# Six expert blocks of a routed layer begun among the last batches' routing, and the blocks' PSUM banks kept in one tile

## The chip, the cores and the metric

The kernel runs on one core of a Trainium2 chip. The metric is the device time of one execution in microseconds. A core has five engines with a queue each: TensorE (PE) for matrix products, with its weight loads (PEld) beside it, VectorE (DVE), ScalarE (ACT), GpSimd (POOL) and SyncE (SP), which issues most DMA transfers. The engines wait for each other by semaphores: a waiting instruction holds everything behind it in its queue. PE's products land in PSUM, which this kernel uses as eight banks of 512 fp32 values per partition; ScalarE and VectorE fetch them from there.

## The reference

A decoder of two layers on x of shape 32 x 100 x 256, each layer with self-attention, cross-attention to a context of 361 rows and a feed-forward part, each followed by a layer normalisation. What matters here is the last part: eight experts, of which each token uses the one with the highest gate.

```python
logits = x_flat @ Wg + bg                       # 3200 tokens, 8 experts
probs = softmax(logits); assignments = argmax(probs)
h = gelu(einsum('nd,edh->neh', x_flat, W1) + b1)
eo = einsum('neh,ehd->ned', h, W2) + b2
selected = take_along_axis(eo, assignments[:, None, None], axis=1)[:, 0, :]
out = probs[token, assignment] * selected
x = layernorm(x + out)
```

## The kernel before

**Slots.** The two layers of attention are planned by hand in slots. `at(slot, place, do)` (L397) files a piece of work under a slot and a place in it, and `run_slots` (L746) issues everything in that order: the scores of the step two slots ahead, then the places -1 and 0, the three turnings of the next step with the places 1, 2, 3 between them, and the sums that close the slot. The order in which instructions are issued is each engine's queue order. A batch of the second layer starts its cross-attention every five slots (`starts`, L467): batch 23 in slot 298, batch 31, the last, in slot 338.

**Routing.** When a batch of the second layer is through its cross-attention, its rows are turned (`r_x_m`), the router gives its logits (L589), and in groups of four batches (at the end two, one, one) VectorE finds each token's expert, counts the tokens of each expert so far (`sofar`, L695) and gives each token a row in a DRAM buffer, `regions`, with one region per expert (L706 to L708). POOL makes the row an integer (L717) and scatters the batch's rows there (L712). The slots of these steps stand in `ROUTING` (L26): for batches 20 to 23 the scatters are in slots 314 to 317, for the last batch in slot 347.

**Blocks.** After the last slot, `block_table` (L727) counts how many blocks of 128 tokens each expert needs and writes for each of 32 blocks its first row in `regions` and its expert into `table`. SP, PE and VectorE read it into registers (`of_four`, L854). Blocks are a software pipeline (L925): in step i, SP asks for the rows and the first matrix of block i + 10 (`xb`, 129 KB, L869; `wb`, 257 KB, L871), PE turns block i + 2 (L877) and ScalarE copies the turned rows to SBUF (`bxT`, L879); PE multiplies block i + 1 by the first matrix (L887), ScalarE applies bias and gelu (`bhT`, L890); PE multiplies block i by the second matrix (L896); VectorE adds bias and residual and takes mean and variance (L899 to L903). ScalarE normalises block i - 3 (L915), POOL scatters it to the output (L712). The last two blocks are normalised on VectorE. The turned rows (`bt`), first products (`bh`) and second products (`bo`) are tiles of the PSUM pool `ps_m`, two of each, opened after the attention's pools are closed:

```python
ps = ps_m.tile([P, NC2, P], F32, tag="t", name=f"bt_{i}")     # L875
ps = ps_m.tile([P, NC2, P], F32, tag="h", name=f"bh_{i}")     # L883
ps = ps_m.tile([P, D], F32, tag="o", name=f"bo_{i}")          # L894
```

A tile is also what waits are made from: the layer that records the program adds a wait wherever an instruction touches a tile that another engine used before.

Of the kernel before, what the change touches and what calls it, by code (L numbers as in the profile page):

```python
# [10 lines left out]
F32 = mybir.dt.float32  # L11
# [7 lines left out]
E = 8  # L19
# [14 lines left out]
FILLS = 23  # L34
NO_TOKEN = 1000000
# [29 lines left out]
def decoder_kernel(ctx: ExitStack, tc: tile.TileContext, a: dict, out: bass.AP):  # L65
# [5 lines left out]
    x_all = state.tile([S, B, ROW], F32, name="x_all")  # L71
    xs = [x_all[:, b, :D] for b in range(B)]
# [3 lines left out]
    table = state.tile([32, 64], I32, name="table")  # L76

# [14 lines left out]

    def centre_and_scale(dst, src, scale):
        nc.vector.tensor_scalar(dst, src, scale[0], scale[1], ALU.subtract, ALU.mult)

    with ExitStack() as att:
# [3 lines left out]
        ps_s = att.enter_context(tc.tile_pool(name="ps_s", bufs=1, space=bass.MemoryType.PSUM))  # L100
        ps_r = att.enter_context(tc.tile_pool(name="ps_r", bufs=4, space=bass.MemoryType.PSUM))
        att.enter_context(tc.manual_schedule())

        def bank(tag):
            return ps_r.tile([P, 512], F32, tag="r", name=f"r_{tag}")
# [12 lines left out]
        nc.vector.tensor_copy(x_all[:, :, D + 1].bitcast(I32), ids)  # L118
# [159 lines left out]

        def score_banks(tag):
            return ps_s.tile([P, NG, 512], F32, tag="s", name=f"sc_{tag}")  # L280
# [376 lines left out]
        place = const.tile([S, B], I32, name="place")  # L657

# [25 lines left out]
        def shares(first, n):  # L684

            top = x_all[:, first:first + n, D]
            nc.vector.tensor_reduce(top, routed["lg"], AX.X, ALU.add)
            nc.vector.reciprocal(top, top)
# [13 lines left out]
        def rows_of(first, n):  # L702
# [5 lines left out]
            nc.vector.tensor_reduce(row[:, first:first + n], ahead, AX.X, ALU.add)  # L708

# [6 lines left out]
        def send(b):  # L716
            nc.gpsimd.tensor_copy(place[:, b:b + 1], row[:, b:b + 1])  # L717
            scatter("regions", out=regions, out_offset=bass.IndirectOffsetOnAxis(ap=place[:, b:b + 1], axis=0),
                    in_=x_all[:, b, :])
# [7 lines left out]
        def block_table():  # L727


            ps = bank("counts")[:, :E]  # L730
            nc.tensor.matmul(ps, lhsT=share_of_block, rhs=sofar, start=True, stop=True)
            n = sm.tile([P, E], F32, tag="tb_n", name="tb_n")
            nc.vector.tensor_scalar(n, ps, 0.5 - 0.5 / P, ROUND, ALU.add, ALU.add)
            nc.vector.tensor_scalar(n, n, ROUND, float(P), ALU.subtract, ALU.mult)
            upto = sm.tile([P, E], F32, tag="tb_upto", name="tb_upto")
            nc.vector.tensor_tensor_scan(upto, ones[:, :E], n, 0.0, ALU.mult, ALU.add)
            past = sm.tile([32, E - 1], F32, tag="tb_past", name="tb_past")
            col = sm.tile([32, 2], F32, tag="tb_col", name="tb_col")
            nc.vector.tensor_scalar(past, upto[:32, :E - 1], c["steps"][:32, 0:1], None, ALU.is_le)
            nc.vector.tensor_reduce(col[:, 1:2], past, AX.X, ALU.add)  # L740
            nc.vector.tensor_scalar(n, n, -1.0, float(B * S), ALU.mult, ALU.add)
            nc.vector.tensor_tensor_reduce(past, past, n[:32, :E - 1], 1.0, c["steps"][:32, 0:1], ALU.mult, ALU.add, col[:, 0:1])
            nc.vector.tensor_copy(rows_by_block[:, 0:64:32], col)
            nc.vector.transpose(table, rows_by_block)

# [79 lines left out]
        b2 = xnT.rearrange("p k b s -> p (k b s)")[:, :E * D].rearrange("p (e d) -> p e d", e=E)  # L825
# [10 lines left out]
        block_table()  # L836

    with ExitStack() as moe:
# [5 lines left out]
        ps_m = moe.enter_context(tc.tile_pool(name="ps_m", bufs=2, space=bass.MemoryType.PSUM))  # L844
        moe.enter_context(tc.manual_schedule())

        y_all = mw.tile([P, BLOCKS, D], F32, name="y_all")
        mv_all = mw.tile([P, BLOCKS, 2], F32, name="mv_all")
        rs_all = mw.tile([P, BLOCKS], F32, name="rs_all")
        shift = mw.tile([P, BLOCKS], F32, name="shift")  # L850
        blocks = [{} for _ in range(BLOCKS)]
        ENG = mybir.EngineType

        def of_four(i, what, engines, most):  # L854

            i += 32 * what
            return nc.values_load_multi_w_load_instructions(
                table[0:1, i:i + 4], engines=engines, min_val=0, max_val=most,
                skip_runtime_bounds_check_because="the table's rows and experts are within these bounds for any counts")[1]

        def load_block(i):
            if i % 4 == 0:
                firsts = of_four(i, 0, (ENG.SP,), (BLOCKS_AT_MOST - 1) * P)
                experts = of_four(i, 1, (ENG.SP, ENG.PE, ENG.DVE), E - 1)
                for t, first, e in zip(blocks[i:i + 4], firsts, experts):
                    t["first"], t["e"] = first, e
            t = blocks[i]
            t["x"] = m16.tile([P, ROW], F32, tag="xb", name=f"xb_{i}")
            nc.sync.dma_start(t["x"], regions[bass.ds(t["first"], P), :])  # L869
            t["w"] = m12.tile([P, WROW], F32, tag="wb", name=f"wb_{i}")  # L870
            nc.sync.dma_start(t["w"], a["experts_1"][bass.ds(t["e"], 1)].rearrange("o p n -> (o p) n"))  # L871

        def turn_block(i):
            t = blocks[i]
            ps = ps_m.tile([P, NC2, P], F32, tag="t", name=f"bt_{i}")  # L875
            for k in range(NC2):
                nc.tensor.transpose(ps[:, k, :], t["x"][:, k * P:(k + 1) * P], ident)  # L877
            t["xT"] = m2.tile([P, NC2, P], F32, tag="bxT", name=f"bxT_{i}")
            nc.scalar.copy(t["xT"], ps)  # L879

        def first_layer(i):
            t = blocks[i]
            ps = ps_m.tile([P, NC2, P], F32, tag="h", name=f"bh_{i}")  # L883
            t["hT"] = m2.tile([P, NC2, P], F32, tag="bhT", name=f"bhT_{i}")
            for m in range(NC2):
# [39 lines left out]
        for i in range(-10, BLOCKS):  # L925
            for f, d in ((load_block, 10), (turn_block, 2), (first_layer, 1)):
                if 0 <= i + d < BLOCKS:
                    f(i + d)
# [89 lines left out]
```

## Time and profile before

| | |
|---|---|
| median of three runs | 1750.93 us (1747.35 to 1752.39) |
| the profiled execution | 1748.03 us |
| its span | 1745.9 us |
| PE busy | 1681.2 us, 96% |
| DVE, ACT, POOL busy | 74%, 52%, 63% |
| last scatter to `regions` issued | at 1658.23 us |
| first turning of a block on PE | at 1663.51 us |
| second product of block 0 and of block 30 | at 1669.67 and 1728.78 us |

The time lies a little above the span because work around the first and last instruction is in it. The profile has several views. The view by stretch gives for each stretch the busy time of each engine and the granted clock of TensorE (1.00 is full speed). The chain that ended last is followed back from the last instruction, each step to what released it. The timeline gives instructions in order of time: start, length, engine, line, operation, output<-inputs, count, and in brackets how long the engine had been idle and what released it. Lines in it are those of the kernel before.

### The profile page before, as it was taken

How to read it: one execution, taken by the hardware profiler on the slowest of the kernel's cores; microseconds unless marked ns; L12 is line 12 of the kernel's file. 1: busy time of each engine (PE TensorE's matmuls, PEld its weight loads, DVE VectorE, ACT ScalarE, POOL GpSimd, SP SyncE). 2: the span in 40 equal slices, each digit the busy share in tenths (PEclk: the TensorE clock that was granted, in tenths of full speed). 3: DMA queues.
4: the chain of work that ended last, by engine and by line, in shares of the span. 5: the costliest groups of instructions: out<-in, count | busy, mean ns of one | idle time of the engine just before them, and what ended most of it. 6: DMA issues, size and time to landing. Idle time of an engine off the chain costs nothing. (4 is left out here: it accounts for less than half of the span.)

```text
span 1745.9 us, 52245 instructions
## 1 busy us (share of the span) xinstructions
PE 1681.2 (96%) x20801; PEld 1302.3 (75%) x20801; DVE 1291.6 (74%) x3784; ACT 912.9 (52%) x2252; POOL 1096.9 (63%) x1657
## 2 busy tenths in 40 slices
PE   8999999999999999999999999999999999999786
PEld 6777777777777777776777777777777777777575
DVE  5677777777777777777667787877777787777655
ACT  3455555555555555555445555555555555554354
POOL 1566666666566666666237667776767667675646
PEclk9999999999999999999999999999999999999888
DMA  4001322332233233310421132000100000100083
GB/s 160 14 22 30 81 76 54 85 81 64 70 81 84 48 82 81 76 30 22 160 63 55 55 103 65 19 20 19 28 19 21 18 22 26 37 27 18 18 257 113
DMA packets 64047, 104.90 MB, mean 60 GB/s; under 512 B 6107, under 2 KB 43485, under 8 KB 63678
## 3 DMA queue, kind: packets, MB, share of 16 engines
q1 hardware_dynamic: 59790, 94.44, 19.7%
q0 software_dynamic: 3584, 6.59, 1.2%
q8 instruction: 165, 2.70, 0.7%
q14 instruction: 76, 0.62, 0.1%
q10 hardware_dynamic: 432, 0.54, 0.1%
HBM read 61.32 MB, written 41.13 MB: 59 GB/s over the span
## 5 line engine op out<-in xcount | busy, mean ns | idle before, releaser
L364 POOL TENSOR_TENSOR pr<-pr,mx_x 100x361 f32<-100x361 f32 x992 | 766.3, 802 | 230.9 <-DVE mx_x L360 222.1
L375 ACT ACTIVATE pT_x<-r_t_x 120x400 f32<-120x400 f32 (+1 forms) x768 | 370.6, 503 | 271.2 <-PE r_t_x L374 269.2
L374 PEld LDWEIGHTS r_t_x<-ident,pr 100*120 100x120 f32 (+1 forms) x3072 | 313.7, 138 | 112.5 <-POOL pr L364 34.0
L374 PE MATMUL r_t_x<-ident,pr 100*120 100x100 f32 (+1 forms) x3072 | 380.7, 252 | 12.3 <-POOL pr L364 11.1
L360 DVE CUSTOM_DVE_ANT_0 pr<-sc_x,dist 100x361 f32<-100x361 f32 x512 | 244.7, 530 | 121.8 <-PE sc_x L277 97.7
L360 DVE CUSTOM_DVE_ANT_0 pr<-sc_x,zero 100x361 f32<-100x361 f32 x512 | 244.6, 530 | 76.7 <-PE sc_x L277 69.5
L277 PE MATMUL sc_x<-kT_x,qz_x 32*100 32x361 f32 x2048 | 221.8, 502 | 8.5 <-DVE mx_x L360 5.2
L89 POOL TENSOR_SCALAR rs_s<-mv_s 100x1 f32<-100x1 f32 x64 | 14.3, 224 | 289.7 <-DVE mv_s L87 261.6
L389 PE MATMUL r_a_x<-pT_x,v_cross 120*32 120x100 f32 (+1 forms) x6144 | 172.2, 252 | 0.0
L318 DVE TENSOR_REDUCE mx_s<-sc_s 100x16 f32<-100x1600 f32 x64 | 116.6, 1823 | 69.8 <-PE sc_s L277 69.8
L477 ACT ACTIVATE kT_x<-r_k,c_columns 128x361 f32<-128x361 f32 x128 | 72.0, 563 | 162.2 <-PE r_k L475 162.2
L389 PEld LDWEIGHTS r_a_x<-pT_x,v_cross 120*32 120x32 f32 (+1 forms) x6144 | 129.9, 110 | 24.1 <-ACT kT_s L424 2.1
L332 ACT ACTIVATE pT_s<-r_t_s 100x400 f32<-100x400 f32 x256 | 112.7, 504 | 30.2 <-PE r_t_s L331 27.6
L321 DVE TENSOR_TENSOR pr_s<-sc_s,mx_s 100x1600 f32<-100x1600 f32 x64 | 116.8, 1824 | 2.2
L331 PE MATMUL r_t_s<-ident,pr_s 100*100 100x100 f32 x1024 | 107.3, 251 | 0.3 <-DVE pr_s L321 0.3
L277 PEld LDWEIGHTS sc_x<-kT_x,qz_x 32*100 32x100 f32 x2048 | 68.3, 160 | 45.2 <-issue 13.8
L484 PE MATMUL r_v<-shared,ctx 128*120 128x256 f32 (+1 forms) x384 | 100.5, 384 | 0.0
L331 PEld LDWEIGHTS r_t_s<-ident,pr_s 100*100 100x100 f32 x1024 | 95.2, 130 | 5.5 <-ACT shared L486 0.6
L486 ACT COPY v_cross<-r_v 120x256 f32<-120x256 f32 x168 | 62.5, 372 | 58.0 <-PE r_v L484 58.0
L268 DVE SCALAR_TENSOR_TENSOR qz_x<-r_qx,qm_x_scale,qm_x_bias 128x400 f32<-128x400 f32 x64 | 37.6, 629 | 71.8 <-PE r_qx L257 71.8
L475 PE MATMUL r_k<-ctx,shared 128*128 128x361 f32 x256 | 88.6, 468 | 1.1 <-DMA ctx<-in_ctxT_dram 1.1
L475 PE MATMUL r_k<-ctx,c_l1x_wk 128*128 128x361 f32 x256 | 89.2, 470 | 0.0
(220 smaller groups left out, 2910.6 us busy)
## 6 DMA issues: line engine op xcount, KB each, us to landing
regions<-no_token SPq DMA_DIRECT2D x23, 1161.0 KB
ctx<-in_ctxT_dram SPq DMA_DIRECT2D x64, 361.0 KB
wb<-in_experts_dram SPq DMA_DIRECT2D x32, 257.0 KB
values_dram<-shared SPq DMA_DIRECT2D x8, 768.0 KB
v_cross<-values_dram SPq DMA_DIRECT2D x8, 768.0 KB
dist<-in_dist_dram SPq DMA_DIRECT2D x32, 141.0 KB
xb<-regions SPq DMA_DIRECT2D x32, 129.0 KB
x_all<-in_x_dram SPq DMA_DIRECT2D x32, 100.0 KB
```

The costliest lines, as they stand in the source:

```text
L277: nc.tensor.matmul(dst, lhsT=qz[rows, p, k, :], rhs=kT[rows, k, :], start=True, stop=True)
L318: nc.vector.tensor_reduce(mx, sg, AX.X, ALU.max)
L321: nc.vector.tensor_tensor(pr, sg, mx.unsqueeze(3).to_broadcast([S, NG, NG, S]), ALU.subtract)
L331: nc.tensor.transpose(pt[:, j, :], t["pr_s"][:, j, g, :], ident[:S, :S])
L332: nc.scalar.activation(t["pT_s"][:, g], pt, AF.Exp)
L360: nc.vector.tensor_tensor_reduce(pr[:, j, :SK], sc[:, j, :], bias, 1.0, LOWEST, ALU.add, ALU.max, mx)
L364: nc.gpsimd.tensor_tensor(pr[:, j, :SK], pr[:, j, :SK], mx.to_broadcast([S, SK]), ALU.subtract)
L374: nc.tensor.transpose(pt[:n, j, :], t["pr_x", g][:, j, k0:k0 + n], ident[:S, :S])
L375: nc.scalar.activation(t["pT_x", g][:n, i], pt[:n], AF.Exp)
L389: nc.tensor.matmul(av[32 * j:32 * j + 32, h, :], lhsT=t["v_x"][:n, i, head(part, j), :], rhs=t["pT_x", part][:n, i, j, :], start=(i == 0), ...
L475: nc.tensor.matmul(ps, lhsT=c[sx + "_wk"][:, k, m * P:(m + 1) * P], rhs=t["ctx"][:, k, :], start=(k == 0), stop=(k == NC2 - 1))
L484: nc.tensor.matmul(ps, lhsT=ctx_b[:, k, k0:k0 + n], rhs=c[sx + "_wv"][:, k, :], start=(k == 0), stop=(k == NC2 - 1))
```

## The change

Six blocks (`BEGUN`) are begun before the attention is over. After batch 23's counting (slot 313), a first table is made of six full blocks among the tokens of the first 24 batches (`table_of_begun`). SP loads their rows and first matrices in slots 321 to 326, one block a slot, into places of `x_all` and `xnT` that are no longer needed (`x_all` now has 128 partitions). Their turnings and first products are put at the places in `BEGINNING`, in slots 338 to 347, in banks of the attention's pool; ScalarE adds the bias there without the gelu. PE and VectorE read their experts' registers in slot 346. After the last slot come the table of the other blocks (`table_of_others`, counted behind the begun ones), then six gelus and six second products (`end_begun`) and the sums (`sum_begun`). Then the pipeline runs over the other 26 blocks. Three of the begun blocks are normalised by ScalarE and stored ahead of block 6's second product, three by VectorE between the blocks' stores.

The attention's two PSUM pools stay open for the blocks. One tile of four banks, `score_banks("blocks")`, holds the turnings (banks 0 and 1) and the first products (banks 2 and 3) of all 26 blocks. Second products take the four rotating banks of the other pool. For the single batches 30 and 31 the row number is made an integer by VectorE, and POOL writes a small constant in its place.

```diff
+BEGUN, BEGIN_WITH = 6, 24
+BEGINNING = (((338, 1), (340, 2)), ((338, 3), (342, 1)), ((339, 1), (343, 3)), ((339, 3), (345, 2)), ((340, 1), (346, 0)), ((341, 1), (347, 1)))
...
-    x_all = state.tile([S, B, ROW], F32, name="x_all")
-    xs = [x_all[:, b, :D] for b in range(B)]
+    x_all = state.tile([P, B, ROW], F32, name="x_all")
+    xs = [x_all[:S, b, :D] for b in range(B)]
...
+    words = xnT.rearrange("p k b s -> p (k b s)")
+    b2 = words[:, :E * D].rearrange("p (e d) -> p e d", e=E)
+    w1_begun = words[:, E * D:E * D + BEGUN * WROW].rearrange("p (i d) -> p i d", i=BEGUN)
...
+    def load_rows_of_block(t):
+        nc.sync.dma_start(t["x"], regions[bass.ds(t["first"], P), :])
+    def load_matrix_of_block(t):
+        nc.sync.dma_start(t["w"], a["experts_1"][bass.ds(t["e"], 1)].rearrange("o p n -> (o p) n"))
+    def turn_rows(t, ps):
+        for k in range(NC2):
+            nc.tensor.transpose(ps[:, k, :], t["x"][:, k * P:(k + 1) * P], t["ident"])
+        nc.scalar.copy(t["xT"], ps)
+    def first_matrix(t, ps, function):
+        for m in range(NC2):
+            for k in range(NC2):
+                n = k * D + m * P
+                nc.tensor.matmul(ps[:, m, :], lhsT=t["w"][:, n:n + P], rhs=t["xT"][:, k, :], start=(k == 0), stop=(k == NC2 - 1))
+        for m in range(NC2):
+            nc.scalar.activation(t["hT"][:, m, :], ps[:, m, :], function, bias=t["w"][:, NC2 * D + m:NC2 * D + m + 1])
+    def second_matrix(t, ps, w):
+        for m in range(NC2):
+            nc.tensor.matmul(ps, lhsT=t["hT"][:, m, :], rhs=w[:, bass.ds(t["e"], 1), m * D:(m + 1) * D].rearrange("p o n -> p (o n)"),
+                             start=(m == 0), stop=(m == NC2 - 1))
+    def share_and_residual(i, ps, pool):
+        t = blocks[i]
+        y = t["y"]
+        nc.vector.tensor_tensor(y, ps, b2[:, bass.ds(t["e"], 1), :].rearrange("p o d -> p (o d)"), ALU.add)
+        nc.vector.scalar_tensor_tensor(y, y, t["x"][:, D:D + 1], t["x"][:, :D], ALU.mult, ALU.add)
+        st = pool.tile([P, 6], F32, tag="st", name=f"st_{i}")
+        nc.vector.bn_stats(st, y)
+        nc.vector.bn_aggr(mv_all[:, i, :], st)
...
+    ps_s = ctx.enter_context(tc.tile_pool(name="ps_s", bufs=1, space=bass.MemoryType.PSUM))
+    ps_r = ctx.enter_context(tc.tile_pool(name="ps_r", bufs=4, space=bass.MemoryType.PSUM))
+    def bank(tag):
+        return ps_r.tile([P, 512], F32, tag="r", name=f"r_{tag}")
+    def score_banks(tag):
+        return ps_s.tile([P, NG, 512], F32, tag="s", name=f"sc_{tag}")
...
+            if n == 1:
+                nc.vector.tensor_copy(place[:, first:first + 1], row[:, first:first + 1])
...
         def send(b):
-            nc.gpsimd.tensor_copy(place[:, b:b + 1], row[:, b:b + 1])
+            if group_of(b)[1] > 1:
+                nc.gpsimd.tensor_copy(place[:, b:b + 1], row[:, b:b + 1])
+            else:
+                nc.gpsimd.memset(between, 0.0)
             scatter("regions", out=regions, out_offset=bass.IndirectOffsetOnAxis(ap=place[:, b:b + 1], axis=0),
-                    in_=x_all[:, b, :])
+                    in_=x_all[:S, b, :])
...
+        def table_of_begun():
+            assert BEGIN_WITH * S - E * (P - 1) > (BEGUN - 1) * P
+            n, upto = blocks_of_experts("begun", 0.5 / P - 0.5, None)
+            nc.vector.tensor_scalar(upto, upto, float(BEGUN), None, ALU.min)
+            nc.vector.tensor_copy(done[:, 0:1], upto[:, 0:1])
+            nc.vector.tensor_tensor(done[:, 1:], upto[:, 1:], upto[:, :E - 1], ALU.subtract)
+            nc.vector.tensor_scalar(n, done, -float(P), float(B * S), ALU.mult, ALU.add)
+            write_table("begun", upto, lambda: n, c["steps"][:, 0:1])
+            nc.vector.tensor_tensor(over, done[:, 1:], done[:, :E - 1], ALU.subtract)
+            nc.vector.tensor_scalar(over, over, float(P), float(B * S), ALU.mult, ALU.add)
+            nc.vector.scalar_tensor_tensor(first_done, done[:, 0:1], float(P), c["steps"][:, 0:1], ALU.mult, ALU.add)
+        def begun_rows():
+            firsts = of_table(0, BEGUN, 0, (ENG.SP,), (BLOCKS_AT_MOST - 1) * P)
+            experts = of_table(0, BEGUN, 1, (ENG.SP,), E - 1)
+            for i, (first, e) in enumerate(zip(firsts, experts)):
+                t = blocks[i]
+                t["first"], t["e"], t["ident"] = first, e, ident
+                t["x"], t["y"] = x_all[:, i, :], x_all[:, BEGUN + i, :D]
+                t["hT"], t["xT"] = slot_of(2 * BEGUN + i), slot_of(3 * BEGUN + i)
+                t["w"] = w1_begun[:, i, :]
+        def begun_experts():
+            for t, e in zip(blocks, of_table(0, BEGUN, 1, (ENG.PE, ENG.DVE), E - 1)):
+                t["e"] = e
+        def load_begun(i):
+            load_rows_of_block(blocks[i])
+            load_matrix_of_block(blocks[i])
+        def of_bank(name):
+            return split(bank(name)[:, :NC2 * P], NC2)
+        def plan_beginning():
+            last = starts(1, BEGIN_WITH - 1)[0]
+            at(last + 15, 1, table_of_begun)
+            at(last + 22, 3, begun_rows)
+            at(last + 48, 3, begun_experts)
+            for i, (turning, first) in enumerate(BEGINNING):
+                at(last + 23 + i, 0, lambda i=i: load_begun(i))
+                at(*turning, lambda i=i: turn_rows(blocks[i], of_bank(f"bt_{i}")))
+                at(*first, lambda i=i: first_matrix(blocks[i], of_bank(f"bh_{i}"), AF.Identity))
+        def end_begun():
+            for t in blocks[:BEGUN]:
+                nc.scalar.activation(t["hT"], t["hT"], AF.Gelu)
+                t["ps"] = bank("bo")[:, :D]
+                second_matrix(t, t["ps"], shared)
+        def sum_begun():
+            for i in range(BEGUN):
+                share_and_residual(i, blocks[i]["ps"], sm)
+                if i == BEGUN // 2 - 1:
+                    margin(0, BEGUN // 2)
+                    scale(0, BEGUN // 2)
+                if i == BEGUN // 2:
+                    shift_of(0, BEGUN // 2)
...
         run_slots()
         nc.scalar.preload_act_table_set("gelu_and_others")
-        block_table()
+        table_of_others()
+        end_begun()
+        sum_begun()
...
+        banks = score_banks("blocks")
...
+            for load in (load_matrix_of_block, load_rows_of_block) if i == BEGUN else (load_rows_of_block, load_matrix_of_block):
+                load(t)
...
         def turn_block(i):
             t = blocks[i]
-            ps = ps_m.tile([P, NC2, P], F32, tag="t", name=f"bt_{i}")
-            for k in range(NC2):
-                nc.tensor.transpose(ps[:, k, :], t["x"][:, k * P:(k + 1) * P], ident)
+            t["ident"] = ident
             t["xT"] = m2.tile([P, NC2, P], F32, tag="bxT", name=f"bxT_{i}")
-            nc.scalar.copy(t["xT"], ps)
+            turn_rows(t, banks[:, i % 2, :NC2 * P].rearrange("p (k s) -> p k s", k=NC2))
         def first_layer(i):
             t = blocks[i]
-            ps = ps_m.tile([P, NC2, P], F32, tag="h", name=f"bh_{i}")
             t["hT"] = m2.tile([P, NC2, P], F32, tag="bhT", name=f"bhT_{i}")
-            for m in range(NC2):
-                for k in range(NC2):
-                    nc.tensor.matmul(ps[:, m, :], lhsT=t["w"][:, k * D + m * P:k * D + (m + 1) * P], rhs=t["xT"][:, k, :],
-                                     start=(k == 0), stop=(k == NC2 - 1))
-            for m in range(NC2):
-                nc.scalar.activation(t["hT"][:, m, :], ps[:, m, :], AF.Gelu, bias=t["w"][:, NC2 * D + m:NC2 * D + m + 1])
+            first_matrix(t, banks[:, 2 + i % 2, :NC2 * P].rearrange("p (k s) -> p k s", k=NC2), AF.Gelu)
         def second_layer(i):
-            t = blocks[i]
-            ps = ps_m.tile([P, D], F32, tag="o", name=f"bo_{i}")
-            for m in range(NC2):
-                nc.tensor.matmul(ps, lhsT=t["hT"][:, m, :], rhs=shared[:, bass.ds(t["e"], 1), m * D:(m + 1) * D].rearrange("p o n -> p (o n)"),
-                                 start=(m == 0), stop=(m == NC2 - 1))
-            y = y_all[:, i, :]
-            nc.vector.tensor_tensor(y, ps, b2[:, bass.ds(t["e"], 1), :].rearrange("p o d -> p (o d)"), ALU.add)
-            nc.vector.scalar_tensor_tensor(y, y, t["x"][:, D:D + 1], t["x"][:, :D], ALU.mult, ALU.add)
-            st = m4.tile([P, 6], F32, tag="st", name=f"st_{i}")
-            nc.vector.bn_stats(st, y)
-            nc.vector.bn_aggr(mv_all[:, i, :], st)
...
+        half = BEGUN // 2
+        for i in range(BEGUN - 10, BLOCKS):
             for f, d in ((load_block, 10), (turn_block, 2), (first_layer, 1)):
-                if 0 <= i + d < BLOCKS:
+                if BEGUN <= i + d < BLOCKS:
                     f(i + d)
-            if 2 < i:
+            if i == BEGUN - 1:
+                for j in range(half):
+                    normalise_on_scalar(j)
+                    store(j)
+            if i < BEGUN:
+                continue
+            if i > BEGUN + 2:
                 normalise_on_scalar(i - 3)
-            if i < 0:
-                continue
             second_layer(i)
             if i == BLOCKS - 1:
                 normalise_on_scalar(i - 2)
                 store(i - 3)
+            if i == BEGUN + 1:
+                margin(half, half)
+                scale(half, half)
             if i % 2:
                 margin(i - 1, 2)
                 scale(i - 1, 2)
-            elif i:
+            elif i > BEGUN:
                 shift_of(i - 2, 2)
-            if 2 < i < BLOCKS - 1:
+            if BEGUN + 1 < i < BEGUN + 2 + half:
+                normalise(i - 2 - half)
+                store(i - 2 - half)
+            if BEGUN + 2 < i < BLOCKS - 1:
                 store(i - 3)
         store(BLOCKS - 3)
```

## The prediction

> **What bounds the kernel now.** I read the share of busy time first (TensorE, PE, 96% of 1745.9 us), then the busy time by stretch, then the chain that ended last, then the rows of one block, then the waits in the built program of each kernel. By stretch (columns: stretch, length, busy PE, weight load, DVE, ACT, POOL with instruction counts, granted TensorE clock, DMA share, GB/s):
>
> ```profile
> 1640.00:1650.00 10.00, 7.34 (x91) 5.61 (x89) 6.70 (x32) 3.64 (x11) 5.17 (x9) 0.94 0.01 2
> 1650.00:1660.00 10.00, 2.80 (x13) 2.24 (x13) 5.36 (x33) 1.82 (x3) 4.27 (x7) 0.50 0.13 36
> 1660.00:1670.00 10.00, 5.21 (x25) 4.79 (x26) 0.00 (x0) 1.92 (x7) 0.00 (x0) 0.54 0.76 207
> 1680.00:1690.00 10.00, 10.00 (x72) 9.22 (x72) 7.91 (x24) 7.42 (x22) 8.29 (x10) 1.00 0.86 259
> ```
>
> Up to about 1640 us PE is full. From 1645 to 1665 it is half idle at half clock: the last batch's routing is a chain of small steps. Then 32 expert blocks run with PE full again. The change wants to fill the hole with six of these blocks. The chain (start, length, what):
>
> ```profile
> 1658.23 2.82 DMA regions<-x_all,place
> ...
> 1662.75 2.65 DMA xb<-regions
> ...
> 1669.67 0.86 PE bo L896 x4
> 1670.54 0.22 PE bt L877 x2
> 1670.76 0.89 PE bh L887 x8
> 1671.65 0.86 PE bo L896 x4
> ...
> 1728.78 0.88 PE bo L896 x4
> ```
>
> A block is 0.22 (turning, bt) + 0.89 (first matrix, bh) + 0.86 (second, bo) = 1.98 us, with nothing between. The second product of block 0 starts at 1669.67, that of block 30 at 1728.78: 59.1 us. Behind it lie 17.1 us of last sums and stores. The rows of one steady block show how PE stays full (start, length, engine, line):
>
> ```profile
> 1693.13 0.74 PEld L896 LDWEIGHTS bo<-shared,bhT 128*128 128x128 f32 x4
> 1693.24 1.03 PE L896 MATMUL bo<-shared,bhT 128*128 x4
> 1693.49 0.62 ACT L890 ACTIVATE bhT<-bh,wb 128x128 f32<-128x128 f32 x2 [0.52 <-PE bh L887]
> 1693.89 0.36 PEld L877 LDWEIGHTS bt<-ident,xb 128*128 128x128 f32 x2
> 1694.01 0.60 ACT L915 ACTIVATE y_all<-y_all,shift,rs_all 128x256 f32<-128x256 f32 x1
> 1694.22 0.97 PEld L887 LDWEIGHTS bh<-bxT,wb 128*128 128x128 f32 x8
> 1694.58 0.37 ACT L879 COPY bxT<-bt 128x256 f32<-128x256 f32 x1
> 1695.47 0.62 ACT L890 ACTIVATE bhT<-bh,wb 128x128 f32<-128x128 f32 x2 [0.52 <-PE bh L887]
> ```
>
> The next turning (1693.89) starts before ScalarE has finished the gelu that runs (1693.49 + 0.62 = 1694.11). The first matrix (1694.22) starts before the copy of the turning just issued (1694.58): it uses the copy made one block earlier.
>
> **Part 1: one tile for the banks, the part that decides.** Before, bt, bh and bo are separate tiles, two of each. Now turnings and first products of all blocks lie in one tile of four banks, opened once. In the program built from the changed kernel I looked up which instruction each semaphore count belongs to:
>
> ```
> turning of block 16      waits for the gelu of block 14         (before: an older turning on PE)
> first matrix of block 15 waits for the copy of turning 16       (before: the copy of turning 15)
> second matrix of 14      waits for an old sum on VectorE        (long done)
> ```
>
> The banks alternate, so no data asks for these waits, but the waits stand in the program. PE and ScalarE now take turns. Latencies from a place where they already do:
>
> ```profile
> 1647.34 0.20 PEld L242 LDWEIGHTS r_x_ox<-ident,o_x 100*128 100x128 f32 x2 [0.69 <-PE r_l L589]
> 1647.37 0.36 PE L242 MATMUL r_x_ox<-ident,o_x 100*128 100x100 f32 x2 [0.63 <-DVE ahead L706]
> 1647.77 0.33 ACT L245 COPY xT_ox<-r_x_ox 128x200 f32<-128x200 f32 x1 [1.92 <-PE r_x_ox L242]
> 1648.14 0.72 PEld L303 LDWEIGHTS r_o_x<-c_l1x_wo,xT_ox 128*100 128x100 f32 x4 [0.60 <-ACT xT_ox L245]
> ```
>
> Turning to copy: 0.43 (1647.34 to 1647.77), 0.45 for 128 columns. Copy 0.37 and 0.04 to the weight load (1647.77 + 0.33 to 1648.14): 0.41. First matrix to gelu: 1694.22 to 1695.47 = 1.25. Gelu 0.62 and 0.04: 0.66. One round is 0.45 + 0.41 + 1.25 + 0.66 = 2.77 us against 1.98. The second matrix (0.86) fits into the 0.36 + 0.66 us after the first matrix; the normalising on ScalarE ends 1.09 after the gelu's start (1693.49 to 1694.58), as the next copy becomes ready (0.66 + 0.45 = 1.11). Bounds: 2.5 if only the wait for the copy cost; 3.5 if the clock falls (below). I take 2.77, because each term is a row.
>
> From second product 6 to 30 there are 24 rounds, the last without a turning (less 0.86): 24 x 2.77 - 0.86 = 65.6 us. Before, 0 to 30 took 59.1. So six blocks leave (6 x 1.98 = 11.9 us gained) and the waits give back 18.4: **+6.5 us**.
>
> **Part 2: the start of the blocks.** New ahead of block 6 is end_begun: six gelus, six second products. The table load (1.28 us at 1655.71) now stands behind block 5's bias step and ends near 1657.6; a gelu of 128x256 takes about 0.6 (the row L915), so product 0 starts near 1658.25. The clock is 0.50 there. Before, PE was busy from 1665.45 and fast from about 1669.5, so 4 us cold: 2.3 products at 1.73, 3.7 at 0.86, end near 1665.5. The last scatter's landing and block 6's rows (before, rows used at 1663.5) are hidden under that, the matrix too, which SP now asks for first. Then the waits again: turning 6, copy, turning 7, copy (2 x 0.86), first matrix to gelu 1.25, 0.52, three normalisings of begun blocks in ScalarE's queue (1.7), copy 8 (0.41), first matrix 7 (0.89): 6.5 us, in which PE does 2.2, so I add 1.0 for half clock. Second product 6 at 1665.5 + 7.5 = 1673.0, against 1669.7: **+3.3**. First rounds at half clock: **+1.5** (0 to 3).
>
> **Part 3: what is put among the routing.** The first block table at slot 313 adds some 16 small VectorE instructions of about 0.17 (rows L733 to L744): 2.7 us, where VectorE is 70 to 80% busy; its queue holds the score maxima, and PE's next scores wait for these. Between 0 and 2.7, I take 1.2. Turnings 0 to 5 (0.22 each) and first matrices (0.89 each): turnings 0 and 1 stand ahead of the last but one score product: +0.4; 2 to 4 and matrix 0 fall into waits of 0.36 to 0.7 for DVE and POOL; turning 5 +0.2; matrix 1 stands ahead of the batch's last sums: +0.9; matrix 2 and its bias step (0.62 on ScalarE, ahead of the copy xT_ox): +0.5; 3 to 5 lie in PE's holes of 2.6 and 1.3 us. PE kept warm gives back about half of the copies of L303, x_m and the router product (1.5, 0.6, 0.8 us cold): -0.9. Sum **+2.3** (0 to 5).
>
> **At nothing.** Six row and matrix loads (386 KB each) in slots 321 to 326, where DMA is 8% busy (1550 to 1600 us): uncovered they would be 2.3 MB at 299 GB/s (the rate from 1672 to 1676), 7.7 us. SP's waits there are for scatters of slots 314 to 317, long landed; the context loads behind them have slots to spare. The later scatters on POOL now wait for these reads, by then eight slots old. Register loads lie in gaps, as the chain has none at them today. Turning the place to integers moves from POOL (0.18) to VectorE; a memset takes POOL's place. The six begun blocks' stores on POOL (0.97 and 0.3 each) now stand between those of the others, in POOL's idle quarter, larger at 2.77 a round. The end (17.1 us) stays.
>
> **Sum.** 6.5 + 3.3 + 1.5 + 2.3 = +13.6 us on a span of 1745.9: 1759.5. The profiled execution took 1748.03, 2.1 more than its span; the median of the runs, 1750.93, is 2.9 above it. Forecast: **1764.5 us**.
>
> **The rule that speaks against staying warm.** Two stretches of the granted clock:
>
> ```profile
> 1644.00:1648.00 4.00, 2.62 (x44) 2.09 (x40) 2.55 (x14) 1.13 (x5) 0.40 (x2) 1.00 0.02 4
> 1648.00:1652.00 4.00, 1.99 (x8) 1.53 (x8) 2.63 (x15) 0.30 (x2) 2.96 (x5) 0.59 0.14 36
> ```
>
> At 66% busy the clock still stands at 1.00, then falls. A round has PE 1.98 of 2.77 busy, 71%. The Trainium skill (TensorE: Matmul & The Clock Gate, "A second HAM failure mode: psum-queue depth-cycling") says that short idles between groups of products, as banks are cycled, make the gate swing. A cold round is about 4.6 us and so full that it warms again; half and half by time, 3.5 a round: 24 x 0.73 = 17.5 more, 1782. By the row, 1764.5. I follow the row, since dense products fill 71%, but give the rule weight.
>
> **Rivals.** (1) The loop is serial and warm: 1764.5, chance 0.60. (2) Serial and the clock swings: 1770 to 1782, 0.22. (3) The routing chain suffers more (Part 3 at 5 to 8 us, cold PE, ScalarE's bias steps ahead of the critical copies): 1768 to 1771, 0.08. (4) Faster: the waits cost nothing because ScalarE answers within PE's other work, a round stays 1.98: second product 6 at 1671 + 2.3 (no waits and no half clock at the start), 24 x 1.98 - 0.2 later, plus 17.1: 1737.7, so 1742.7. For it: the gelu ends only 0.22 after the turning starts today. Against: the copy cannot come before its own turning. It decides below 2.2 us a round, where the gain of 11.9 outweighs the start; 0.07. (5) A draw, between 2.2 and 2.35 a round: 0.03.
>
> **Numbers.** What this kernel's measurement can tell from no change is about 0.3%, 5.3 us. Cases 1 to 3 are slower: 0.90; 0.07 faster; 0.03 the same. Range 1757 (a round of 2.5) to 1782 (clock swinging throughout); it leaves out case 4 and the tails.
>
> **What would show it.** In the after profile: about 2.8 us from one second product to the next, PE near 70% busy between 1680 and 1740, first matrices released by ScalarE's copy, turnings by the gelu; second product 6 near 1675; the granted clock tells case 1 from 2. I am wrong if PE has no idle time in the rounds, or if the last scatter leaves more than 5 us late.

## The result: slower, with the rounds as long as the waits make them

| | before | after |
|---|---|---|
| median of the runs | 1748.36 us (1747.35 to 1752.39, six runs) | 1765.65 us (1761.08 to 1767.29, six runs) |
| the profiled execution, its span | 1748.03, 1745.9 us | 1761.08, 1759.0 us |
| last scatter to `regions` issued | 1658.23 | 1659.00 |
| second products of the begun blocks | | 1659.50 to 1667.5 |
| second product of block 6 (before: block 0) | 1669.51 | 1673.81 |
| second product of block 30 | 1728.61 | 1742.17 |

The changed kernel takes 1.009 times as long, 95% interval 1.0077 to 1.0103. The forecast was 1764.5 us, on a span of 1759.5. (Starts of products are here those of the timeline; the chain of the kernel before, from which 1669.67 and 1728.78 were taken, has the same two products 0.16 later.)

The view by stretch of the changed kernel (columns as before):

```profile
1640.00:1650.00 10.00, 9.27 (x118) 8.07 (x116) 6.47 (x29) 5.63 (x17) 3.97 (x7) 1.00 0.01 2
1650.00:1660.00 10.00, 6.48 (x45) 5.62 (x46) 6.54 (x41) 5.36 (x17) 5.45 (x10) 0.90 0.12 32
1660.00:1670.00 10.00, 8.98 (x35) 7.11 (x34) 8.13 (x24) 1.72 (x6) 1.13 (x2) 0.76 0.71 212
1670.00:1680.00 10.00, 6.92 (x44) 5.31 (x44) 4.42 (x12) 4.57 (x13) 4.84 (x7) 1.00 0.99 332
1680.00:1690.00 10.00, 7.97 (x47) 5.66 (x45) 6.36 (x19) 5.22 (x15) 5.46 (x7) 1.00 0.51 181
```

The hole of PE from 1650 to 1670 is filled: 6.5 and 9.0 us busy against 2.8 and 5.2, at a clock of 0.90 and 0.76 against 0.50 and 0.54. But from 1680 to 1690, where PE had 72 products in ten microseconds, it now has 47. All engines do less there, and the clock is at 1.00: PE waits. One round of the changed kernel, from the timeline (start, length, engine, line):

```profile
1702.55 1.03 PE L132 MATMUL r_bo<-shared,bhT 128*128 x4
1702.80 0.62 ACT L128 ACTIVATE bhT<-sc_blocks,wb 128x128 f32<-128x128 f32 x2 [1.30 <-PE sc_blocks L126]
1703.32 0.60 ACT L1035 ACTIVATE y_all<-y_all,shift,rs_all 128x256 f32<-128x256 f32 x1
1703.48 0.20 PEld L119 LDWEIGHTS sc_blocks<-ident,xb 128*128 128x128 f32 x2 [0.30 <-ACT bhT L128]
1704.01 0.37 ACT L120 COPY bxT<-sc_blocks 128x256 f32<-128x256 f32 x1
1704.43 0.97 PEld L126 LDWEIGHTS sc_blocks<-bxT,wb 128*128 128x128 f32 x8 [0.76 <-ACT bxT L120]
1705.32 0.73 PEld L132 LDWEIGHTS r_bo<-shared,bhT 128*128 128x128 f32 x4
1705.43 1.03 PE L132 MATMUL r_bo<-shared,bhT 128*128 x4
```

The turning (1703.48) comes after the gelu (1702.80 + 0.62 = 1703.42), and the first matrix (1704.43) after the copy of the turning just made (1704.01 + 0.37 = 1704.38). In the kernel before, the turning started while the gelu ran, and the first matrix ahead of the copy. From one second product to the next are 2.88 us (1702.55 to 1705.43), against 1.98.

### The profile page after: what moved, and what is told of

It reads as the page before. It is cut to its first block, busy times and chain, and to the rows that moved or that the text cites. A ratio compares the mean times of both kernels' runs of the same rounds, so it can differ in the third digit from the quotient of the medians.

```text
span 1759.0 us, 52227 instructions
## 1 busy us (share of the span) xinstructions
PE 1689.9 (96%) x20803; PEld 1298.5 (74%) x20803; DVE 1295.7 (74%) x3803; ACT 913.0 (52%) x2255; POOL 1096.0 (62%) x1655
## 4 chain that ended last, share of the span: by engine, by line
PE 76%; DVE 15%; POOL 4%; issue 3%; DMA 1%; ACT 1%; SPq 0%; POOLq 0%; ACTq 0%; DVEq 0%
PE r_t_x L435 13%; PE sc_x L341 10%; PE r_k L536 8%; PE r_v L545 7%; PE r_a_x L450 6%; DVE pr L421 6%; PE r_t_s L392 4%; PE r_o_x L364 3%; POOL pr L425 3%; PE r_qx L321 2%; PE r_o_s L364 2%; PE sc_s L341 2%; PE r_a_s L399 2%; DVE pr_s L382 2%; DVE mx_s L379 2%
```

## Experiments

The first four versions ran on one chip, the last three on another. Each ratio is to the kernel before on the same chip (median 1748.19 us on the first, 1750.13 on the second).

### A tile for each block's banks

In the blocks, a turning gets a tile of its own (two banks in turn), a first product too; nothing else changes.

```diff
+        ps_m = moe.enter_context(tc.tile_pool(name="ps_m", bufs=2, space=bass.MemoryType.PSUM))
...
+        def block_bank(kind, i):
+            return ps_m.tile([P, 512], F32, tag=kind, name=f"b{kind}_{i}")[:, :NC2 * P].rearrange("p (k s) -> p k s", k=NC2)
...
-        banks = score_banks("blocks")
...
-            turn_rows(t, banks[:, i % 2, :NC2 * P].rearrange("p (k s) -> p k s", k=NC2))
+            turn_rows(t, block_bank("t", i))
...
-            first_matrix(t, banks[:, 2 + i % 2, :NC2 * P].rearrange("p (k s) -> p k s", k=NC2), AF.Gelu)
+            first_matrix(t, block_bank("h", i), AF.Gelu)
```

(`ps_s` is closed with the attention, so that the eight banks suffice. There are two banks of each kind in turn, as in the changed kernel: only the borders of the tiles differ.)

> The changed kernel, but the turnings and the first products of blocks 6 to 31 get one tile for each block (two banks for turnings, two for first products, taken in turn) in place of parts of one tile of four banks. Theory (the shared tile makes PE and ScalarE take turns): a round falls from 2.88 to about 1.98 us, so from second product 6 to 30 about 47 us instead of 68.4, the start of the blocks loses another 1 to 2 us, and the span is about 1736 to 1740 us: 8 us below the kernel before, 22 below the changed one. Rival (ScalarE's own work, 0.37 + 0.62 + 0.60 a block with its gaps, sets the round): a round stays above 2.5 us and the span above 1750. Rival (the clock would have fallen in a denser stretch too): a round between 1.98 and 4 with a granted clock below 0.9.

Measured: 1739.02 us (1738.28 to 1741.55), 0.9942 of the kernel before (0.9925 to 0.9958). Its timeline:

```profile
1706.81 1.03 PE L132 MATMUL r_bo<-shared,bhT 128*128 x4
1707.06 0.63 ACT L128 ACTIVATE bhT<-bh,wb 128x128 f32<-128x128 f32 x2
1707.46 0.36 PEld L119 LDWEIGHTS bt<-ident,xb 128*128 128x128 f32 x2
1707.58 0.60 ACT L1038 ACTIVATE y_all<-y_all,shift,rs_all 128x256 f32<-128x256 f32 x1
1707.79 0.97 PEld L126 LDWEIGHTS bh<-bxT,wb 128*128 128x128 f32 x8
...
1708.79 1.03 PE L132 MATMUL r_bo<-shared,bhT 128*128 x4
```

Nothing lies between the products, the brackets of idle time are gone, and 21 of 24 rounds take 2.02 us or less, most of them 1.98. From second product 6 to 30 are 49.5 us (1672.89 to 1722.41) in place of 68.4, and from the last scatter to second product 6 are 10.5 in place of 14.4 (mean of two profiles of the changed kernel, the second below): 18.9 + 3.9 = 22.8 us that the one tile costs. The medians lie 26.6 apart. No trace shows the other 3.8: the changed kernel's median lies 4.6 above its profiled execution, the median here 2.5 below. Without the shared tile the change makes the kernel faster. Both rivals fall: ScalarE answers within the short round, and the granted clock is 1.00 in each stretch of ten from 1670 to 1720.

Three rounds are longer, 2.54, 2.92 and 2.71 us. The first has the normalisings of three begun blocks ahead of a copy in ScalarE's queue. In the other two ScalarE idles, and what it waited for I could not find:

```profile
1688.31 0.37 ACT L120 COPY bxT<-bt 128x256 f32<-128x256 f32 x1 [1.23 <-PE r_bo L132]
1689.84 0.63 ACT L128 ACTIVATE bhT<-bh,wb 128x128 f32<-128x128 f32 x2 [1.16 <-issue]
```

The turning that this copy takes had been made at 1686.23, and the matrix of this gelu at 1686.44. It stays open.

### Two tiles of two banks

```diff
+        ps_m = moe.enter_context(tc.tile_pool(name="ps_m", bufs=1, space=bass.MemoryType.PSUM))
...
-        banks = score_banks("blocks")
+        turn_banks, first_banks = (ps_m.tile([P, 2, 512], F32, tag=k, name=f"b{k}") for k in "th")
...
+            turn_rows(t, turn_banks[:, i % 2, :NC2 * P].rearrange("p (k s) -> p k s", k=NC2))
...
+            first_matrix(t, first_banks[:, i % 2, :NC2 * P].rearrange("p (k s) -> p k s", k=NC2), AF.Gelu)
```

> The changed kernel, but with two tiles of two banks: one for all turnings, one for all first products. Theory: the costly waits are those between the two kinds (a turning waiting for the gelu, a first matrix waiting for the copy of the next turning), so this alone brings the round back to 1.98 to 2.1 us and the span to within 3 us of the kernel with a tile for each block, 1736 to 1742. Rival (each kind waits for its own neighbour too: a turning for the copy of the turning before, a first matrix for the gelu of the block before): the round stays between 2.3 and 2.9 and the span above 1746.

Measured: 1743.66 us (1742.70 to 1744.08), ratio 0.9972 (0.996 to 0.9985). The profiled span, 1741.3 us, is in the range of the first theory, though not every round is: 17 of the 24 rounds take 2.05 us or less, the other seven 2.2 to 3.0; 51.8 us from second product 6 to 30. So the costly waits are those between the kinds, a turning for a gelu and a first matrix for the next turning's copy. The waits within one kind (a first matrix for the last gelu) cost nothing as long as ScalarE is on time, but lengthen a slip, as here:

```profile
1688.40 1.03 PE L132 MATMUL r_bo<-shared,bhT 128*128 x4
1689.77 0.63 ACT L128 ACTIVATE bhT<-bh,wb 128x128 f32<-128x128 f32 x2 [1.14 <-PE bt L119]
1690.44 0.97 PEld L126 LDWEIGHTS bh<-bxT,wb 128*128 128x128 f32 x8 [1.03 <-issue]
1691.44 1.03 PE L132 MATMUL r_bo<-shared,bhT 128*128 x4
```

The gelu was late, and the next first matrix starts after 1.03 us of idle time, 0.04 behind that gelu's end (1689.77 + 0.63 = 1690.40).

### The kernel before, with one tile

```diff
+        ps_b = moe.enter_context(tc.tile_pool(name="ps_b", bufs=1, space=bass.MemoryType.PSUM))
...
+        banks = ps_b.tile([P, NG, 512], F32, tag="s", name="sc_blocks")
...
-            ps = ps_m.tile([P, NC2, P], F32, tag="t", name=f"bt_{i}")
+            ps = banks[:, i % 2, :NC2 * P].rearrange("p (k s) -> p k s", k=NC2)
...
-            ps = ps_m.tile([P, NC2, P], F32, tag="h", name=f"bh_{i}")
+            ps = banks[:, 2 + i % 2, :NC2 * P].rearrange("p (k s) -> p k s", k=NC2)
```

> The kernel before, but the turnings and the first products of its 32 blocks lie in one tile of four banks; nothing else is changed. Theory: 31 rounds lengthen by 0.85 to 0.9 us each, so 26 to 28 us more: about 1775 us. Rival (the waits alone cost little, and the slower rounds of the changed kernel come from its other order of work, for example from the begun blocks' normalisings and stores): less than 8 us more, below 1757.

Measured: 1780.48 us (1777.94 to 1785.19), ratio 1.0187 (1.0163 to 1.0211): 32 us more, so the waits do it alone, without any of the other edits. The rounds are the 2.88 us of the changed kernel, and the start is worse than I had expected:

```profile
1671.39 1.91 PE L899 MATMUL bo<-shared,bhT 128*128 x4
1676.12 1.91 PE L899 MATMUL bo<-shared,bhT 128*128 x4
1679.94 1.03 PE L899 MATMUL bo<-shared,bhT 128*128 x4
1682.82 1.03 PE L899 MATMUL bo<-shared,bhT 128*128 x4
```

The first two rounds, 4.73 and 3.82 us, are at half clock (0.59 from 1670 to 1680). From second product 0 to 30 are 88.5 us against 59.1: +29.4, of which 2.8 are these two rounds; 3.1 more lie between the last scatter and second product 0 (14.4 against 11.3).

### The normalising on VectorE

```diff
-            nc.scalar.activation(y, y, AF.Identity, bias=shift[:, i:i + 1], scale=rs_all[:, i:i + 1])
+            centre_and_scale(y, y, (mv_all[:, i, 0:1], rs_all[:, i:i + 1]))
```

> The changed kernel, but the normalising of each block, 0.60 us on ScalarE, is done on VectorE, so that ScalarE has only the copy and the gelu of a block (1.0 us of a round of 2.88). Theory (a round is a chain through PE and ScalarE, and the normalising lies beside it except for the last 0.08 us ahead of the copy): a round falls by 0.05 to 0.1 us, the start by up to 1.7, so 2 to 4 us in all, about 1762. Rival (ScalarE's load is the bound): 0.6 us of each of the rounds, 14 to 16 us, about 1750. Rival (VectorE becomes late instead): slower than the changed kernel.

Measured: 1763.61 us (1761.07 to 1766.32), ratio 1.0079 (1.006 to 1.0098); the interval overlaps that of the changed kernel. ScalarE's load is not the bound. Taking 0.60 us from it leaves the round at 2.88 us (one of the 24 took 2.93):

```profile
1703.17 0.20 PEld L119 LDWEIGHTS sc_blocks<-ident,xb 128*128 128x128 f32 x2 [0.30 <-ACT bhT L128]
1703.70 0.37 ACT L120 COPY bxT<-sc_blocks 128x256 f32<-128x256 f32 x1 [0.58 <-PE sc_blocks L119]
1704.12 0.97 PEld L126 LDWEIGHTS sc_blocks<-bxT,wb 128*128 128x128 f32 x8 [0.76 <-ACT bxT L120]
1705.12 1.03 PE L132 MATMUL r_bo<-shared,bhT 128*128 x4
```

From turning to copy are 0.53 us here too, though ScalarE has been free for 0.58. So the 0.53 are latency, and my expectation that the normalising delays the copy by 0.05 to 0.1 was wrong. Here too the first two rounds were cold, 4.73 and 3.87 us.

### The first table two slots later

This starts from the kernel with a tile for each block's banks.

```diff
-            at(last + 15, 1, table_of_begun)
+            at(last + 17, 1, table_of_begun)
```

> The kernel with a tile for each block's banks, but the first block table is made two slots later, where VectorE stood idle for 2.7 us (1542.37 to 1545.07 in that kernel's trace) waiting for a projection on PE. In the trace of the changed kernel every instruction up to 1523 us stands 1.47 us ahead of the kernel before, and after the table 1.02 behind it: 2.49 us for its 18 small VectorE instructions. Theory (they cost their whole length only because VectorE's queue had no gap there): the delay of the routing falls from 2.5 to under 0.5 us, the time by 2 to 2.5, to about 1737. Rival (the counts product takes one of four banks in rotation on PE, and that shift is what costs): the delay stays above 1.5 us wherever the table is put, and the time near 1739.

The scatters tell what the table costs, since a trace's distance to the kernel before is constant over long stretches. The changed kernel stood 1.47 us ahead up to 1523 us, in instructions that both kernels have, before anything of the change. Its table, from the timeline:

```profile
1527.94 0.16 DVE L803 TENSOR_SCALAR begun_n<-r_begun 128x8 f32<-128x8 f32 x1
...
1530.36 0.15 DVE L834 SCALAR_TENSOR_TENSOR first_done<-done,c_columns 128x1 f32<-128x1 f32 x1
...
1530.74 0.23 DVE L350 RECIPROCAL rc_x<-r_n_x 100x16 f32<-100x16 f32 x1
```

That reciprocal stands at 1529.72 in the kernel before: 1.02 behind in place of 1.47 ahead, 2.49 us for 16 small instructions (not 18) that take 2.57 in all. VectorE has no gap there, and everything behind waits.

Measured with the table two slots later: 1735.52 us (1734.35 to 1738.99), ratio 0.9921 (0.9907 to 0.9934). With the table where it was, on the other chip, it was 0.9942 (0.9925 to 0.9958); the intervals meet, so the traces have to decide. At the scatters from 1620 us on, the table adds 0.15 us here and 2.2 there. These 2.0 us are the table's part of the 3.5 between the medians. The count product still takes its bank in the rotation, so the rival falls. The table's instructions took longer here, 4.1 us, and delayed the next query scaling by about 1.5. Further on nearly all of that was taken back, and only 0.3 of the 2.49 at the earlier place. This is the fastest version: 0.8% below the kernel before.

### The begun work behind the routing

This too starts from the kernel with a tile for each block's banks.

```diff
-                at(*turning, lambda i=i: turn_rows(blocks[i], of_bank(f"bt_{i}")))
-                at(*first, lambda i=i: first_matrix(blocks[i], of_bank(f"bh_{i}"), AF.Identity))
...
         table_of_others()
+        for i in range(BEGUN):
+            turn_rows(blocks[i], of_bank(f"bt_{i}"))
+            first_matrix(blocks[i], of_bank(f"bh_{i}"), AF.Identity)
         end_begun()
```

> The kernel with a tile for each block's banks, but the turnings and first matrices of the six begun blocks stand behind the second block table, after all routing, and not among its slots. It measures what their place among the routing is worth. Theory (they lie in holes of PE there, at a cost of 1.3 us to the chain, given back by a warmer clock): the last scatter leaves 0 to 1 us earlier or at the same time, and the six blocks then take 6 x 1.11 = 6.7 us at full clock, up to 13 at half, ahead of the six second products; the rows of block 6 arrive under them, so 7 to 11 us more than the kernel with its own tiles: 1746 to 1750, the gain gone. Rival (PE would have waited for block 6's rows anyway): less than 4 us more.

Measured: 1757.50 us (1754.94 to 1759.20), ratio 1.0051 (1.0034 to 1.0068), 18.5 us more than with the work among the routing (1739.02, on the other chip); 7 to 11 were expected. Its view by stretch, and rows of PE and ScalarE from the timeline:

```profile
1640.00:1650.00 10.00, 8.06 (x84) 6.18 (x83) 5.88 (x28) 3.57 (x11) 3.84 (x7) 0.67 0.01 2
1650.00:1660.00 10.00, 5.53 (x23) 4.12 (x23) 5.44 (x33) 2.26 (x5) 4.76 (x9) 0.50 0.11 32
1660.00:1670.00 10.00, 8.35 (x34) 7.14 (x35) 0.96 (x7) 2.66 (x9) 0.66 (x1) 0.50 0.64 187
```

```profile
1661.87 0.63 PE L119 MATMUL r_bt<-ident,x_all 128*128 128x128 f32 x2
1663.05 2.08 PE L126 MATMUL r_bh<-x_all,xnT 128*128 128x128 f32 x8 [0.55 <-ACT x_all L120]
1664.92 0.64 PE L119 MATMUL r_bt<-ident,x_all 128*128 128x128 f32 x2
...
1677.42 5.45 PE L132 MATMUL r_bo<-shared,x_all 128*128 x24
1682.70 1.03 PE L132 MATMUL r_bo<-shared,bhT 128*128 x4
1683.56 0.38 PE L119 MATMUL bt<-ident,xb 128*128 128x128 f32 x2
1685.89 1.58 ACT L1039 ACTIVATE x_all<-x_all,shift,rs_all 128x256 f32<-128x256 f32 x3 [7.00 <-DVE shift L151]
1687.78 2.08 PE L126 MATMUL bh<-bxT,wb 128*128 128x128 f32 x8 [3.83 <-ACT bxT L120]
```

A begun block takes 3.05 us (1661.87 to 1664.92), not 1.11: half clock, and each matrix waits for its own turning's copy. Block 8's matrix then waits 3.8 us, and block 7's gelu with it, since ScalarE is held by the begun blocks' normalisings (1685.89), whose sums came late. I had left out both the copy and this. Against the version with the work among the routing, 12.6 us more lie between the last scatter and second product 6 (23.0 for 10.5) and 3.8 more from there to product 30 (53.3 for 49.5). The routing itself is longer too: from the scatter at 1633 us to the last one are 24.77 us in the kernel before, 24.84 with the work among the routing, 26.22 here with PE at half clock.

### The changed kernel once more

> The changed kernel unaltered, once more. Its profiled execution (1761.1 us) was the shortest of six, whose median is 1765.7, and it stood 1.47 us ahead of the kernel before already at 1050 us, before anything of the change. Theory (the difference between executions lies partly in the first 100 us, as in the kernel with its own tiles, whose granted clock was 0.91 from 60 to 80 us and which stood 3.4 us behind from there on, and partly in a cold start of the blocks, as in the kernel with the normalising on VectorE, whose first two rounds took 4.73 and 3.87 us): a profile of about 1765 shows one of these or both, with rounds of 2.88 us. Rival (the rounds themselves vary): rounds above 3.0 us over a longer stretch.

Measured: 1764.81 us (1761.26 to 1766.71). The profile again fell on the shortest execution (1761.26), so no trace tells what the 3 to 6 us more of most others are. Their clocks give a hint. Of the changed kernel's ten executions, three took 1761 us at a mean granted clock of 0.994 or 0.995, and seven took 1764 to 1767 at 0.991 or 0.992. The version with the normalising on VectorE has the same two groups, and its profile is of a long one (1766.32 us, 0.991), with cold first rounds. A cold start of the blocks may so be the usual case for the changed kernel too; that is not shown. The profile repeats the rest: rounds of 2.88 us and one of 3.16, 68.4 us from second product 6 to 30, a span of 1759.2. At 1452 us it stood 0.30 ahead of the kernel before, not 1.47.

## Why the prediction was right, step by step

Both profiles of the changed kernel against the kernel before, in us (in brackets the second profile). The first row is what the trace shows before the first table. It is not due to the change, as it differs between two executions of the same program; the last section has its origin.

| | predicted | measured |
|---|---|---|
| ahead of the first table | | -1.5 (-0.3) |
| routing, up to the last scatter | +2.3 | +2.2 (+2.2) |
| last scatter to second product 6 | +3.3 | +3.5 (+2.6) |
| second product 6 to 30 (+6.5, and +1.5 for first rounds at half clock) | +8.0 | +9.3 (+9.3) |
| the end | 0 | -0.5 (-0.5) |
| sum | +13.6 | +13.1 (+13.3) |

**Part 1, the round: mechanism right, size short.** Both waits stand in the timeline as they were read from the program, and taking away the shared tile alone removes them. Of the four terms three hold to 0.02 us: 0.42 (predicted 0.41), 1.24 (1.25), 0.68 (0.66). The term of turning to copy was mis-sized: 0.53 for 0.45, which I had scaled from a turning of 100 columns. A round of 2.88 for 2.77 is 2.6 us in 24 rounds, and one round of 3.16 adds 0.3; the missing turning ahead of block 30's product gives back 0.96 and not 0.86. So the waits cost 2.8 us more than forecast, and the +1.5 for cold first rounds, which these two executions did not have, hid half of it.

**Part 2, the start: right in sum, its terms not all.** Product 0 of the begun blocks starts 0.5 us behind the last scatter, where I had them together. The six products took 8.0 and 7.1 us in the two profiles, for 7.25 (1658.25 to 1665.5). The ramp from their end to second product 6 took 6.3 us in both, for 6.5 and 1.0 for half clock: it ran at full clock, so in these two executions neither the 1.0 nor the +1.5 for the first rounds was due. They do exist: where the start was cold, in the one-tile version of the kernel before and with the normalising on VectorE, the first two rounds cost 2.8 us together, and a cold round took the 4.73 us for which I had estimated 4.6.

**Part 3, the routing: the sum right, its terms not.** I took 1.2 us for the table, between 0 and 2.7; it cost 2.49, of which 0.3 were taken back later, because VectorE's queue was full just there. The turnings and first matrices, estimated at +2.0 with 0.9 given back by a warm PE, left 0.07 in the routing, together with what else changed there. In the trace the shift rises by 0.4 at the turnings 0 and 1 and by 0.9 at matrix 1, as worked out; the further 0.7, for turning 5 and matrix 2, is not in it at the next scatter (1650 us). Then it falls again by 1.3. Some 0.9 of this lie where the router product and the copies run at full clock, as forecast. The other 0.4 I had put at nothing: VectorE now makes the last row number an integer, and from that number to its scatter are 0.65 us (1658.35 to 1659.00) in place of 1.03 (1657.20 to 1658.23). Two errors of about 1 us cancelled, which is luck.

**What was costed at nothing.** Besides that move and an end 0.5 us shorter, no row shows a cost of the six loads, the registers or POOL's stores; none was tested by itself.

**The rivals.** The clock did not swing. From 1670 to 1740 us the granted clock is 1.00 in each stretch of ten, with PE at work 1.98 of 2.88 us. I had given this 0.22 on what the Trainium skill reports (TensorE: Matmul & The Clock Gate, "A second HAM failure mode: psum-queue depth-cycling") of one bf16 kernel, in which short idles between groups of products, with banks cycled in each iteration, make the gate swing. In these fp32 rounds, with banks cycled too, it did not; here the row that showed 1.00 at 66% busy was the better guide. The faster case (0.07) needed a round below 2.2 us. Its time, 1742.7, is near what the versions without the costly waits take: 1743.7 with two tiles, 1739.0 with a tile for each block.

**From span to time.** The profiled executions lie 2.1 us above their spans, as I took it, and the forecast span of 1759.5 meets the measured 1759.0. That the time fits as well is partly luck. By medians the change costs 17.3 us (1748.36 to 1765.65), not 13.6. I had started from a median of 1750.93, of three runs; that of six is 2.6 lower. Most other runs of the changed kernel lie 3 to 6 us above the profiled ones, where I had allowed 2.9, and what they do longer is not shown.

## What to carry to other kernels

Where the layer that records a program makes waits per tile, several banks in one tile are one resource, and alternating between them doesn't double-buffer: give each buffer a tile, and look up in the built program whose end a turning or a matrix waits for before counting what its pipeline gains. Work that fills a hole of PE can be worth more than its length (18 us here for 6.7 us of products at full clock): placed behind the hole, it ran at half clock, waited for its own copies, and its late sums held up what followed. But its bookkeeping must be put where the engine that does it has a gap: 2.5 us of tiny VectorE instructions cost their full length in one slot and almost nothing two slots later.

## What the runs showed of the hardware that I had not expected

**The clock dips in some executions and not in others.** Instructions that all versions share stood up to 4.1 us apart at 1340 us, between executions of different versions, and kept their distance for hundreds of microseconds. The distances arise at two places. Between 60 and 80 us the granted clock was 0.91 in three versions (a tile for each block's banks, the normalising on VectorE, the later table), and these stood 1.8 to 2.0 us behind the kernel before from there on (the kernel before, then the first of the three; columns as in the first view):

```profile
60.00:80.00 20.00, 16.96 (x260) 13.00 (x258) 12.56 (x37) 10.65 (x27) 12.59 (x17) 1.00 0.09 28
```

```profile
60.00:80.00 20.00, 16.96 (x246) 13.16 (x245) 11.68 (x33) 10.24 (x25) 12.32 (x17) 0.91 0.09 28
```

Between 900 and 920 us the clock dipped in six of the nine profiles, that of the kernel before among them. The other three held 1.00, and moved ahead of the kernel before by 1.7 us just there. Here one program shows both, the changed kernel in its first and its second profile:

```profile
900.00:910.00 10.00, 8.19 (x93) 6.59 (x92) 6.64 (x15) 5.87 (x15) 4.45 (x7) 1.00 0.03 10
```

```profile
900.00:910.00 10.00, 8.19 (x81) 6.16 (x80) 6.22 (x12) 4.96 (x13) 4.03 (x6) 0.85 0.01 4
```

None of the edits touches these stretches, so I take both dips for draws of an execution. For the second the two profiles show it; for the first no program was seen both ways. To compare two traces, take such a constant distance off first.

**A 0.17 us instruction that took 1.21.** In the version with the later table, two of its VectorE instructions were stretched while POOL multiplied `pr`:

```profile
1539.15 3.03 POOL L425 TENSOR_TENSOR pr<-pr,mx_x 100x361 f32<-100x361 f32 x4
...
1540.33 1.21 DVE L805 TENSOR_SCALAR begun_n<-begun_n 128x8 f32<-128x8 f32 x1
1541.57 0.64 DVE L809 TENSOR_TENSOR_SCAN begun_upto<-ones,begun_n 128x8 f32<-128x8 f32 x1
1542.24 0.17 DVE L827 TENSOR_SCALAR begun_upto<-begun_upto 128x8 f32<-128x8 f32 x1
```

At the earlier place, where POOL was idle, both took 0.17. The second ends at 1542.21, just behind POOL's last product (1542.18). This fits what the Trainium skill says of the two engines (SBUF — State Buffer, "Who interferes with whom"): some VectorE instructions share a pair of ports with GpSimd, as an exclusive lock held for a whole instruction. No run here tested it by itself, so the cause is not shown.
